# Layer 1's matrices: the second product by even and odd frequencies on row halves, and the root beside it by seed and refinement

## The chip, the cores and the metric

The kernel runs on one core of a Trainium2 chip. The metric is the device time of one execution in microseconds (us), the median over the runs. The engines are TensorE (PE in the profile; PEld is its weight load), VectorE (DVE), ScalarE (ACT), GpSimd (POOL) and SyncE (SP), whose queue issues most DMAs.

## The reference, cut to what matters

Two layers follow each other. Layer 0 takes x of shape 4 x 256 x 256 x 64 through a layer norm, a pointwise product, a two-dimensional Fourier transform, a pointwise layer with gelu, the inverse transform and a depthwise convolution. Layer 1 takes a moving average along the first spatial axis, and filters the rest by one complex matrix for each of 64 channels:

```python
eps = 1e-3                                       # layer 0's norm: (x - mu) * rsqrt(var + eps)
trend = _moving_average(x, KERNEL)               # along T = 256
seasonal = x - trend
xf = jnp.fft.rfft(seasonal, axis=1)
xs = xf[:, :M]                                   # M = 128 frequencies
W = w_real + 1j * w_imag                         # 64 matrices of 128 x 128
ys = jnp.einsum('bmnc,cmk->bknc', xs, W)
filt = jnp.fft.irfft(yf, n=T, axis=1)            # yf is ys with zeros behind it
return trend + filt
```

All of layer 1 is linear in its input, so for each channel c it is one real 256 x 256 matrix: the average, plus (rfft after the removal of the average) x W[c] x (irfft). The kernel computes these 64 matrices itself, since W is an input.

## The kernel before, in words

The whole program is fp32 and runs in stages: a first stage with layer 0's forward transform and most of layer 1's matrices, then the spectral stage, the stages that mix spectrum and convolution, and at the end layer 1 itself, one product per channel with the matrices loaded back from DRAM.

*Forward chunks.* `forward_h` handles chunks of 1024 numbers a partition, 32 for each of the four images. `load` (fl) issues four DMAs into `xt`, which has three buffers. `square` (fq, ScalarE), `add` (fr, VectorE, L283: total), `less_mean` (fR, ScalarE, L288 and L289: mean and sq) and `variance` (fm, VectorE, L294: var) give the statistics; `start_root` (fM) decides on the kind of root, and `root` (fp) makes rstd = (var)^-1/2; `scaled` (fx, GpSimd, L410) multiplies; `halves` (fa, VectorE, L582) and `quarters` (fb, VectorE, L602) form sums and differences; `halves_h` (fh0 and fh1, L609) forms two more, in the first chunks one on GpSimd and one on VectorE, in `xb`, which has one buffer. `transform` (y0, y1, L615) multiplies on TensorE as pairs of 64 columns, and `evict` (yt0, yt1, L633) copies to `yt` and stores to `y_d`.

*Roots.* In this stage `joint["whole"]` is True, and `root` is one GpSimd power (L383) on 128 x 16. Elsewhere in the program it can be a seed from VectorE (L315, an integer operation on the bits of var) and a refinement that alternates between ScalarE and GpSimd in `square_seed`, `first_step`, `square_step` and `root` (fA, fB, fC, fp), called spread.

*Matrices.* `first` (v, L1409 and L1410) multiplies a channel's 128 x 128 real and imaginary weights with tables `f1` and `f2` of 512 columns into one bank. `between` (vc, ScalarE, L1414) copies the bank to `vs`. `second` (mm, L1421) multiplies the two halves of vs with the inverse tables `icr` and `ici` of 256 columns: four products into one bank. `third` (mt, VectorE, L1432) adds the average `avgT` to the bank and stores to `m_d`. 56 channels go this way. The last eight go by halves (hv, hc, hm, ht) beside the spectral stage.

*Order.* TensorE, VectorE, ScalarE and GpSimd run in the order in which the program issues, written out by hand as lists of operations with offsets. `starting` walks the list `FIRST` for 17 periods, each with two chunks and three channels, and from the second period on also a piece of the weight preparation (`prepare`). `BETWEEN` adds five channels and the first steps toward the spectral stage. `do` pulls what an operation follows (`FOLLOWS`), and `make_room` pulls what frees a PSUM bank; there are eight banks, and `NEEDS` says how many an operation takes.

Of the kernel before, what the change touches and what calls it, by code (L numbers as in the profile page):

```python
# [11 lines left out]
F32 = mybir.dt.float32  # L12
I32 = mybir.dt.int32
AF = mybir.ActivationFunctionType
ALU = mybir.AluOpType
# [4 lines left out]
P = 128  # L20
N = 256
C = 64
# [16 lines left out]
def _tables():  # L39

    n = np.arange(N)
# [26 lines left out]
    fr, fi = fr[:, both_halves], fi[:, both_halves]  # L68

# [31 lines left out]
    for par in range(2):  # L101
# [20 lines left out]
        "avgT": fold(avg.T[both_halves]),  # L122
    }
# [13 lines left out]
def conv_seq_kernel(ctx: ExitStack, tc: tile.TileContext, a: dict, tables: bass.AP, out: bass.AP):  # L137
    nc = tc.nc
# [16 lines left out]
    NEEDS = dict(m0=2, m1=2, u=2, s=2, gm=2, em=2)  # L155
# [93 lines left out]
    joint = {"on": False, "open": None, "whole": True}  # L249
# [4 lines left out]
    def statistics(index, src, name, side):  # L254
# [53 lines left out]
        def start_root(j):  # L308
            s = get(j)
            s["whole", side] = joint["whole"] or side == 0 and not joint["on"]  # L310
            s["spread", side] = joint["on"]
            cols = s["cols", side] = None if s["whole", side] else cols_of(s)
            if cols is not None:
                var, seed = s["var"][:, cols], s["seed"][:, cols]
                nc.vector.tensor_scalar(  # L315
                    seed.bitcast(I32), var.bitcast(I32), -0.5, float(0x5F3759DF), ALU.mult, ALU.add
                )
# [1066 lines left out]
    def matrices(pool):  # L1384
# [4 lines left out]
        def table1(name):  # L1389
            return t1[:, _COLS[name][0] - _L1_START : _COLS[name][1] - _L1_START]  # L1390

        f1, f2, icr, ici = (table1(k) for k in ("f1", "f2", "icr", "ici"))
        avgT = table1("avgT")
        CG = 4
# [9 lines left out]
        def first(c):  # L1404
            if c % CG == 0 and c + CG < C:
                load(c + CG)
            ps = pss[c] = bank(f"ps_v_{c}")
            wr, wi = (w[c - c % CG, k][:, c % CG, :] for k in range(2))
            nc.tensor.matmul(ps, wr, f1, start=True, stop=False)  # L1409
            nc.tensor.matmul(ps, wi, f2, start=False, stop=True)  # L1410
# [6 lines left out]
        def second(c):  # L1417
            vs, ps = vss.pop(c), bank(f"ps_m_{c}")
            for t in range(2):
                for r, ic in enumerate((icr, ici)):  # L1420
                    nc.tensor.matmul(  # L1421
                        ps[:, t * N : (t + 1) * N],
                        vs[:, r, t * P : (t + 1) * P],
                        ic,
                        start=r == 0,
                        stop=r == 1,
                    )
            pss[c] = ps

        def third(c):  # L1430
            mt = pool.tile([P, 2, N], F32, tag="mt", name=f"mt_{c}", bufs=3)
            nc.vector.tensor_tensor(mt.rearrange("p t n -> p (t n)"), avgT, pss.pop(c), ALU.add)  # L1432
            free(f"ps_m_{c}")
            nc.sync.dma_start(m_d[c], mt)
# [36 lines left out]
        ops = {"v": first, "vc": between, "mm": second, "mt": third}  # L1471
# [78 lines left out]
    def is_late(j):  # L1550
# [14 lines left out]
        st0 ft0 | st1 ft1 st0 | vc v | mm vc | mt mm | hc hv | hm hc | ht hm  # L1565
# [13 lines left out]
    for line in FOLLOWS.replace("\n", "|").split("|"):  # L1579
# [33 lines left out]
        v:1 mm:-2 fl:1 fM fr fm y0:-2 y1:-2 v:2 mm fq:1 fx:-1 fp fh1:-1 fh0:-1 fm:1 vc:1 yt0:-2 fq:1  # L1613
        y1:-1 mt:-2 fx yt1:-2 fb:-1 mt:-3 fb mt fh1 yt0:-1 fp:1 vc:1 mm:-4 fa:-1 fr:1 fl:2 vc y0:-1
        v:1 fR fR:1 yt1:-1 fh0:-1 fM:1 fa
# [9 lines left out]
    MATRICES = {"v", "vc", "mm", "mt"}  # L1625
# [53 lines left out]
    def period(n):  # L1679
        if any(n - k in chunk_at for k in range(7)):  # L1680
            names = FULL if n < B * FWD + 4 else MIXED if n < CONV_FROM else CONV
        else:
            names = SPECTRUM
        joint["on"], joint["whole"] = names is FULL, names is SPECTRUM
# [17 lines left out]
    with in_order, ExitStack() as right:  # L1702
        with (
# [7 lines left out]
            with ExitStack() as early:  # L1711
# [15 lines left out]
                for k, names in enumerate(BETWEEN, C - BESIDE - len(BETWEEN)):  # L1727
                    do("v", k)
                    do("vc", k)
                    do("mt", k - 1)  # L1730
                    for op, at in names:
                        do(op, S0 - 1 + at)
                do("mt", C - BESIDE - 1)
# [66 lines left out]
```

## Time and profile before

| quantity | value |
|---|---|
| median of 2 runs | 4286.2 us (4285.57 to 4286.83) |
| profiled execution, its own time | 4282.18 us |
| its span, first to last instruction | 4280.0 us |
| mean granted TensorE clock | 0.987 |
| busy over the span: PE, PEld, DVE, ACT, POOL | 96%, 54%, 81%, 69%, 74% |
| first and last start of the second product (L1421) | 17.4 and 315.3 us |
| L1409 / L1410 / L1421, records and median of one | 112 of 592 ns / 112 of 592 ns / 448 of 379 ns |
| L1414 / L1432, instructions and median of one | 56 of 568 ns / 56 of 680 ns |
| L383 over the whole program, instructions and median of one | 41 of 2905 ns |

An fp32 product shows as two records, each with a weight load of its own. [...]in a row of records the next one starts earlier than the last ends, so the time of many is read from their starts. The line numbers are those of the kernel before; in the changed kernel the same functions lie a few lines lower. In the order of time, a line has its start, the time until its end, the engine, line, operation, tiles and number of instructions merged, and in brackets the idle time of the engine before it and what ended it.

### The profile page before, as it was taken

The page shows a single profiled execution, that of the slowest core. Times are in us where ns is not written, and L with a number is a line of the kernel's source. Part 1 is how long each engine was busy: PE and PEld are TensorE (multiplying, and loading weights), DVE is VectorE, ACT ScalarE, POOL GpSimd, SP SyncE. Part 2 cuts the span into 40 slices and gives each one's busy share as a digit, 9 for nine tenths or more (in the row PEclk, how much of TensorE's full clock was granted, in tenths as well). Part 3 has the DMA queues.
Part 4 walks back from the last instruction along what each step waited for, and adds up shares of the span by engine and source line. Part 5 has one row for each costly group of instructions (what it writes and reads, how often), then busy time and mean ns, then how long its engine had stood idle before and what let it go on. Part 6 is the DMA issues. An engine that isn't in the chain of part 4 may idle for free.

```text
span 4280.0 us, 67389 instructions
## 1 busy us (share of the span) xinstructions
PE 4123.3 (96%) x22443; PEld 2329.5 (54%) x22443; DVE 3453.5 (81%) x5234; ACT 2962.3 (69%) x5409; POOL 3174.2 (74%) x3156
## 2 busy tenths in 40 slices
PE   8999999889999999899999999999998899999999
PEld 4544444345555555455555556666665566654444
DVE  6968999889999999899999878888886799962222
ACT  3438988778888887788888777888885466641221
POOL 6869999789999988899988877888886688840000
PEclk9999999999999999999999999999999999999999
DMA  6664555535555545445554333444433544439895
GB/s 192 213 192 132 158 159 165 170 99 138 139 138 138 138 138 141 125 132 140 141 141 133 100 106 101 110 108 123 109 99 101 165 114 114 118 109 368 344 342 226
DMA packets 763904, 655.26 MB, mean 153 GB/s; under 512 B 46413, under 2 KB 657695, under 8 KB 755240
## 3 DMA queue, kind: packets, MB, share of 16 engines
q1 hardware_dynamic: 726696, 583.84, 47.0%
q10 hardware_dynamic: 36864, 67.13, 4.1%
q8 instruction: 180, 2.95, 0.3%
q14 instruction: 164, 1.34, 0.1%
HBM read 364.81 MB, written 286.00 MB: 152 GB/s over the span
## 4 chain that ended last, share of the span: by engine, by line
PE 47%; DVE 8%; DMA 2%; POOL 2%; ACT 1%; issue 1%; SPq 0%; DVEq 0%; POOLq 0%; ACTq 0%
PE ps_o L1504 9%; PE ps_h_c L1166 5%; PE ps_p L750 4%; PE ps_h_c L1180 4%; PE ps_f_c L1283 4%; PE ps_s_c L1041 3%; PE ps_hh_c L1166 3%; PE ps_z L805 3%; PE ps_u L856 2%; PE ps_x L725 2%; PE ps_t_c L1088 2%; PE ps_ft_c L1308 2%; PE ps_hh_c L1180 2%; PE ps_zt L823 1%; PE ps_y L615 1%
## 5 line engine op out<-in xcount | busy, mean ns | idle before, releaser
L770 DVE TENSOR_TENSOR g<-ps_p,g 128x512 f32<-128x512 f32 x1040 | 703.0, 683 | 127.7 <-ACT g L764 109.4
L781 POOL TENSOR_TENSOR g<-g 128x512 f32<-128x512 f32 (+1 forms) x520 | 674.1, 1312 | 92.8 <-ACT g L775 84.9
L775 ACT ACTIVATE g<-g,b_fc 128x1024 f32<-128x1024 f32 (+1 forms) x520 | 595.2, 1145 | 1.7 <-DVE g L770 1.6
L750 PE MATMUL ps_p<-xs,wp 64*128 64x512 f32 (+1 forms) x2080 | 562.2, 615 | 7.0 <-DVE g L770 3.8
L1166 PE MATMUL ps_h_c<-td,wc_main 128*128 128x256 f32 x2048 | 500.5, 387 | 3.7 <-DVE g L770 1.4
L1504 PE MATMUL ps_o<-xc,mt 128*128 128x512 f32 x1024 | 441.2, 594 | 2.6 <-DVE oc L1518 2.6
L1166 PEld LDWEIGHTS ps_h_c<-td,wc_main 128*128 128x128 f32 x2048 | 372.6, 192 | 99.3 <-issue 32.1
L764 ACT COPY g<-ps_p 128x512 f32<-128x512 f32 (+1 forms) x520 | 298.5, 589 | 163.3 <-PE ps_p L750 80.7
L1276 ACT ACTIVATE h_c<-h_c,b_conv 128x1024 f32<-128x1024 f32 x256 | 296.5, 1160 | 158.1 <-DVE h_c L1245 53.8
L1518 DVE TENSOR_SCALAR oc<-ps_o,b_fp 128x512 f32<-128x512 f32 x128 | 93.6, 749 | 348.0 <-DMA out_dram<-oc 177.4
L1516 ACT ACTIVATE oc<-ps_o,b_fp 128x512 f32<-128x512 f32 x128 | 86.4, 686 | 359.4 <-PE ps_o L1504 202.8
L1128 POOL TENSOR_TENSOR td<-tt 128x512 f32<-128x512 f32 x256 | 326.9, 1298 | 10.0
L1504 PEld LDWEIGHTS ps_o<-xc,mt 128*128 128x128 f32 x1024 | 194.9, 191 | 248.3 <-issue 236.2
L609 POOL TENSOR_TENSOR xb<-xt 128x512 f32<-128x512 f32 x224 | 284.9, 1279 | 54.9 <-DVE xt L602 36.6
L750 PEld LDWEIGHTS ps_p<-xs,wp 64*128 64x128 f32 x2080 | 191.7, 186 | 235.7 <-issue 84.2
L805 PE MATMUL ps_z<-g,w_tp 128*64 128x512 f32 x1024 | 284.7, 616 | 25.8 <-POOL g L781 13.9
L1322 DVE TENSOR_TENSOR st<-x_c,ps_ft_c 128x256 f32<-128x256 f32 x512 | 260.5, 599 | 36.9 <-PE ps_ft_c L1308 36.8
L725 PEld LDWEIGHTS ps_x<-tab,yb 128*64 128x64 f32 x4064 | 232.7, 137 | 95.7 <-issue 38.3
L1180 PE MATMUL ps_h_c<-td,wc_half 64*128 64x256 f32 (+1 forms) x2048 | 278.9, 396 | 2.3 <-POOL td L1132 1.0
L615 PE MATMUL ps_y<-xb,tab 128*64 128x512 f32 x1024 | 270.6, 614 | 10.8 <-POOL xb L609 9.2
L1283 PE MATMUL ps_f_c<-h_c,w_fp 128*64 128x512 f32 x1024 | 266.1, 614 | 15.2 <-ACT h_c L1276 15.2
L1041 PE MATMUL ps_s_c<-uc_c,tab 64*128 64x512 f32 x1024 | 260.4, 612 | 16.6 <-DVE uc_c L990 11.2
(201 smaller groups left out, 9588.2 us busy)
## 6 DMA issues: line engine op xcount, KB each, us to landing
y_d<-yt SPq DMA_DIRECT2D x256, 256.0 KB, 3.6
yb<-y_d SPq DMA_DIRECT2D x256, 256.0 KB, 4.2
u_d<-ut SPq DMA_DIRECT2D x256, 256.0 KB, 3.6
x_c<-in_x_dram SPq DMA_DIRECT2D x512, 128.0 KB, 3.6
x_d<-st SPq DMA_DIRECT2D x128, 512.0 KB, 5.1
xc<-x_d SPq DMA_DIRECT2D x64, 1024.0 KB, 8.3
out_dram<-oc ACTq DMA_DIRECT2D x256, 256.0 KB, 5.7
xt<-in_x_dram SPq DMA_DIRECT2D x504, 128.0 KB, 2.5
```

Source lines behind the costliest of these rows:

```text
L725: nc.tensor.matmul(ps[r * C : (r + 1) * C, j * N + t * P : j * N + (t + 1) * P], blk[:, t, k, r * C : (r + 1) * C], tb[:, t, :], start=Tru ...
L750: nc.tensor.matmul(ps[:, :nf], wp[rows, cols], rhs[rows], start=True, stop=r == 1 or not pr["special"],)
L770: nc.vector.tensor_tensor(gt[:, i], re, gt[:, 1], op)
L775: nc.scalar.activation(g, g, AF.Gelu, bias=b_fc[:, half : half + 1])
L781: nc.gpsimd.tensor_tensor(g[:, 0], g[:, 0], g[:, 1], op)
L805: nc.tensor.matmul(ps[r * C : (r + 1) * C, :nf], w_tp, d[:, :nf], start=True, stop=True)
L1041: nc.tensor.matmul(pss[i], tb[i * C : (i + 1) * C], uc[i * C : (i + 1) * C, ::-1, 1 - r, :] if down else uc[i * C : (i + 1) * C, :, r, :], ...
L1128: tt_(new[:, k : k + 3 : 2], a_c, nb_e, op)
L1166: nc.tensor.matmul(product(j, k, par), wc_main[:, par, k, :], td[:, k, slots(j)].rearrange("p j q -> p (j q)"), start=k in (0, 1, 3), stop ...
L1180: nc.tensor.matmul(product(j, k, par)[:, dst.start * Q : dst.stop * Q], wc_half[lo : lo + C, k, :], td[lo : lo + C, k, src].rearrange("p j ...
L1283: nc.tensor.matmul(ps[par * C : (par + 1) * C], w_fp, gs[j][:, :, par, i0 : i0 + 2, :].rearrange("p r j q -> p r (j q)"), start=True, stop ...
L1504: nc.tensor.matmul(ps[:, :nf], mts[i // CM][:, i % CM, t, to * P : (to + 1) * P], xc[:, t, :, :, i, :], start=t == 0, stop=t == 1,)
```

## The change

The irfft's table has a symmetry: half a turn on (T = 256, row n + 128), even frequencies repeat and odd ones change sign. The change uses it in the second product of the 56 channels.

- A table `icp` holds the inverse's first 128 columns with the rows of even frequencies first and those of odd ones after them; it is loaded with the others.
- `first` takes the weights' even and odd columns apart (`s::2`), so that the bank's rows 0 to 63 hold even frequencies and 64 to 127 odd ones: four products of 64 weight columns, in pairs.
- `second` makes eight products of 64 rows by 128 columns, even ones into one bank and odd ones into another (`NEEDS` 2 for mm).
- `odd` (mo) copies the odd bank to SBUF on ScalarE. `third` (mt) adds the even bank, repeated, to the average on VectorE. `fourth` (mu) adds the odd part to one half on VectorE and subtracts it from the other on GpSimd, and stores.
- The roots of the first stage (35 chunks) become seed and spread refinement, by `joint["first"]`, which the first spectral period sets to False.
- `FIRST` is a new list, with mo and mu and with fA, fB, fC in it.

```diff
+    by_parity = np.concatenate([np.arange(0, P, 2), np.arange(1, P, 2)])
+    icp = np.concatenate([icr[by_parity, :P], ici[by_parity, :P]], axis=1)
...
-    NEEDS = dict(m0=2, m1=2, u=2, s=2, gm=2, em=2)
+    NEEDS = dict(mm=2, m0=2, m1=2, u=2, s=2, gm=2, em=2)
...
-    joint = {"on": False, "open": None, "whole": True}
+    joint = {"on": False, "open": None, "whole": False, "first": True}
...
-            s["whole", side] = joint["whole"] or side == 0 and not joint["on"]
-            s["spread", side] = joint["on"]
+            s["whole", side] = joint["whole"] or side == 0 and not (joint["on"] or joint["first"])
+            s["spread", side] = joint["on"] or joint["first"]
...
-            nc.tensor.matmul(ps, wr, f1, start=True, stop=False)
-            nc.tensor.matmul(ps, wi, f2, start=False, stop=True)
+            for k, f in enumerate((f1, f2)):
+                for s in range(2):
+                    nc.tensor.matmul(
+                        ps[s * C : (s + 1) * C],
+                        w[c - c % CG, k][:, c % CG, s::2],
+                        f,
+                        start=k == 0,
+                        stop=k == 1,
+                    )
...
         def second(c):
-            vs, ps = vss.pop(c), bank(f"ps_m_{c}")
+            vs = vss.pop(c)
+            pss[c] = [bank(f"ps_m{k}_{c}")[:, :N] for k in "eo"]
             for t in range(2):
-                for r, ic in enumerate((icr, ici)):
-                    nc.tensor.matmul(
-                        ps[:, t * N : (t + 1) * N],
-                        vs[:, r, t * P : (t + 1) * P],
-                        ic,
...
+                for r in range(2):
+                    for s in range(2):
+                        rows = slice(s * C, (s + 1) * C)
+                        nc.tensor.matmul(
+                            pss[c][s][:, t * P : (t + 1) * P],
+                            vs[rows, r, t * P : (t + 1) * P],
+                            icp[rows, r],
+                            start=r == 0,
+                            stop=r == 1,
+                        )
+
+        def odd(c):
+            turns[c] = pool.tile([P, 2, P], F32, tag="odd", name=f"odd_{c}", bufs=2)
+            nc.scalar.copy(turns[c].rearrange("p t n -> p (t n)"), pss[c].pop())
+            free(f"ps_mo_{c}")
 
         def third(c):
-            mt = pool.tile([P, 2, N], F32, tag="mt", name=f"mt_{c}", bufs=3)
-            nc.vector.tensor_tensor(mt.rearrange("p t n -> p (t n)"), avgT, pss.pop(c), ALU.add)
-            free(f"ps_m_{c}")
-            nc.sync.dma_start(m_d[c], mt)
+            mt = pool.tile([P, 2, 2, P], F32, tag="mt", name=f"mt_{c}", bufs=3)
+            even = pss.pop(c)[0].rearrange("p (t n) -> p t n", t=2)
+            nc.vector.tensor_tensor(
+                mt,
+                avgT.rearrange("p (t h n) -> p t h n", t=2, h=2),
+                even.unsqueeze(2).to_broadcast([P, 2, 2, P]),
+                ALU.add,
+            )
+            free(f"ps_me_{c}")
+            turns[c] = mt, turns[c]
+
+        def fourth(c):
+            mt, o = turns.pop(c)
+            nc.vector.tensor_tensor(mt[:, :, 0], mt[:, :, 0], o, ALU.add)
+            nc.gpsimd.tensor_tensor(mt[:, :, 1], mt[:, :, 1], o, ALU.subtract)
+            nc.sync.dma_start(m_d[c], mt.rearrange("p t h n -> p t (h n)"))
...
-        st0 ft0 | st1 ft1 st0 | vc v | mm vc | mt mm | hc hv | hm hc | ht hm
+        st0 ft0 | st1 ft1 st0 | vc v | mm vc | mo mm | mt mo | mu mt | hc hv | hm hc | ht hm
...
     FIRST = numbered("""
-        v:1 mm:-2 fl:1 fM fr fm y0:-2 y1:-2 v:2 mm fq:1 fx:-1 fp fh1:-1 fh0:-1 fm:1 vc:1 yt0:-2 fq:1
-        y1:-1 mt:-2 fx yt1:-2 fb:-1 mt:-3 fb mt fh1 yt0:-1 fp:1 vc:1 mm:-4 fa:-1 fr:1 fl:2 vc y0:-1
-        v:1 fR fR:1 yt1:-1 fh0:-1 fM:1 fa
+        mt:-3 fl:1 mu:-3 mm:-2 v:1 fm fM y0:-2 y1:-2 v:2 mm fx:-1 fA fB fC fq:1 fx fp fh0:-1 mt:-2
+        fh1:-1 mu:-2 yt1:-2 yt0:-2 vc:1 mo:-2 fM:1 mo mt mu y1:-1 fr:1 fm:1 fb:-1 mo:-3 fB fb fh1
+        fa:-1 vc:1 fh0:-1 fR:1 mm:-4 fr:1 yt0:-1 fA:1 fC:1 fp:1 fl:2 fR vc y0:-1 fq:1 v:1 yt1:-1 fa
     """)
...
-                    do("mt", k - 1)
+                    do("mu", k - 1)
```

## The prediction

> **What bounds the kernel now.** The page's busy shares (TensorE 96%) mix stages, so I first asked for the busy time in stretches of 20 us, to find where the matrices' lines (L1409 to L1434) run: 10 to 316 us and nowhere else. Only this stage can change: 17 periods of two forward chunks and three channels, then a tail of five channels up to the first spectral product at 316.7 us. A middle stretch reads (columns: busy us and count of TensorE, weight loads, VectorE, ScalarE, GpSimd; granted clock, DMA share, GB/s):
>
> ```profile
> 120.00:140.00 20.00, 19.54 (x71) 9.96 (x70) 18.07 (x23) 9.09 (x19) 17.65 (x10) 1.00 0.65 196
> ```
>
> Three engines look full, so the second view is the order of time on VectorE, over one period:
>
> ```profile
> 124.67 1.28 DVE L582 TENSOR_TENSOR xb<-xt 128x512 f32<-128x512 f32 x2
> 125.99 1.29 DVE L602 TENSOR_TENSOR xt<-xb 128x512 f32<-128x512 f32 x2
> 127.20 1.28 DVE L1432 TENSOR_TENSOR mt<-t,ps_m 128x512 f32<-128x512 f32 x2
> 128.40 0.88 DVE L609 TENSOR_TENSOR xb<-xt 128x512 f32<-128x512 f32 x1
> 129.20 1.21 DVE L283 TENSOR_REDUCE total<-xt 128x16 f32<-128x1024 f32 x1
> 130.95 1.25 DVE L294 TENSOR_REDUCE var<-sq 128x16 f32<-128x1056 f32 x1 [0.55 <-ACT sq L289]
> 132.12 1.30 DVE L582 TENSOR_TENSOR xb<-xt 128x512 f32<-128x512 f32 x2
> 133.46 1.29 DVE L602 TENSOR_TENSOR xt<-xb 128x512 f32<-128x512 f32 x2
> 134.78 0.69 DVE L609 TENSOR_TENSOR xb<-xt 128x512 f32<-128x512 f32 x1
> 135.64 1.22 DVE L283 TENSOR_REDUCE total<-xt 128x16 f32<-128x1024 f32 x1 [0.16 <-DMA xt<-in_x_dram]
> 137.40 1.25 DVE L294 TENSOR_REDUCE var<-sq 128x16 f32<-128x1056 f32 x1 [0.55 <-ACT sq L289]
> 138.57 0.68 DVE L1432 TENSOR_TENSOR mt<-t,ps_m 128x512 f32<-128x512 f32 x1
> ```
>
> VectorE starts the next instruction where the last one ends; its only waits are 0.55 us for ScalarE's mean (L289), twice, and 0.16 for a load. Start to start: halves 1.32 and quarters 1.32 a chunk, L609 0.61 to 0.80, total with its wait 1.75, variance 1.17, and 0.60 for each mt: 2 x 6.27 + 3 x 0.60 = 14.3 us. The period from 251.43 to 265.96, which holds no weight preparation, measured 14.53; this one, with 0.96 of preparation, 15.58. VectorE sets the period. TensorE is second: a record of 512 columns takes 0.427 us (two records per fp32 product), so a channel costs 1.71 + 1.71 and a chunk's ps_y 1.71, 13.7 us a period, and up to 14.5 with the 0.15 us seen at each change of tile shape.
>
> Third, the waits on loads and on the power:
>
> ```profile
> L383 POOL TENSOR_TENSOR rstd<-var,minus_half 128x16 f32<-128x16 f32 x33 | 101.5, 3075 | 34.3 <-DVE var L294 34.0
> 64.93 1.28 POOL L609 TENSOR_TENSOR xb<-xt 128x512 f32<-128x512 f32 x1 [2.93 <-DVE xt L602]
> 68.54 0.47 SPq L569 DMA_DIRECT2D xt<-in_x_dram  x1
> 71.51 1.06 ACT L279 ACTIVATE sq<-xt 128x1024 f32<-128x1024 f32 x1 [2.16 <-DMA xt<-in_x_dram]
> ```
>
> The root is 2.9 to 3.1 us of GpSimd a chunk. A chunk's load goes into the buffer that GpSimd's L609 of three chunks before releases: L609 ends at 66.21 and ScalarE's square, which waits for the load, starts at 71.51, 5.3 us later. ScalarE has nothing else to do then, so today it costs nothing.
>
> Fourth, what an idle TensorE costs afterwards:
>
> ```profile
> 302.50 3.68 PE L615 MATMUL ps_y<-xb,tab 128*64 128x512 f32 x8 [4.56 <-POOL xb L609]
> 263.81 1.94 PE L615 MATMUL ps_y<-xb,tab 128*64 128x512 f32 x8
> 3285.26 1.11 PE L1088 MATMUL ps_t_c<-ident,xn_c 128*128 128x128 f32 x4 [3.22 <-POOL xn_c L410]
> 3244.93 0.66 PE L1088 MATMUL ps_t_c<-ident,xn_c 128*128 128x128 f32 x4 [2.97 <-POOL xn_c L410]
> ```
>
> The same eight records take 1.94 after work and 3.68 after 4.56 us of idleness. In the stretches of the order of time that I read, every gap over 3.4 us was followed by half speed; gaps of 2.8 to 3.3 went either way, and nearly all shorter ones were harmless.
>
> **What the Trainium skill says.** "TensorE: Matmul & The Clock Gate" (Part 1) gives the same: about 3.4 us of idleness halve the clock, about 3.4 us of work restore it; the trace agrees (3.68 against 1.94). "TensorEngine Tiling (Array Packing)" (Key Properties; PSUM Pressure) says that different tiles run in parallel, and that row tiles must write different banks, which the even and odd banks do; here 16 records of 64 rows by 256 columns (L1180, 2009.70) take 2.00 us and 32 of L725 take 1.92, hence pairs in parallel. "VectorE: DVE Perf Modes" (tier table) keeps fp32 tensor_tensor at its lowest rate, so an SBUF sum of 256 columns costs what L602's 128x256 row shows, 0.42 (0.34 start to start).
>
> **The change part by part.** *First product*: two products become four of 64 columns in pairs. L615 has this shape: 1.71 a channel, as before. Cost 0.
>
> *Second product*: four of 256 columns become eight of 128 on row halves, 16 records in pairs. At 0.107 (128 columns) to 0.116 (L725) a pair: 0.9 us instead of 1.71. Lower bound of the gain 0 (pairs in series), upper 0.85; I take 0.8, 2.4 a period. It lies off VectorE's chain, so the stage gains nothing from it; it becomes idleness.
>
> *Sums*: VectorE's mt stays 512 wide (0.60), then adds 128x256, 0.34: 3 x 0.34 = 1.02 a period on the chain. ScalarE copies the odd bank, 0.37 (L1453) x 3; GpSimd subtracts 128x256, of which the trace has no row: between 0.64 (half of L609) and 1.28 (all of it); I take 0.67, 2.0 a period.
>
> *Root*: VectorE gets the seed (128x16; L315 shows 0.16 to 0.18, about 0.13 start to start) twice, 0.26. The power goes; in its place come five small ScalarE and four small GpSimd operations in turn. The later stage shows the chain (tile newton_c, from 905.4 to 908.5): 0.25 to 0.45 a hop, 3.0 us in all. GpSimd waits in order through it, so its 2.9 us are not freed.
>
> VectorE's floor therefore rises by 1.28: 15.8 a period without preparation, 16.9 with.
>
> *New order*: two of these chains now hang on other things. In the changed order ScalarE has, inside the root of chunk e+2, the square of chunk e+3 with its load wait; and ahead of the root of e+3 it has the eviction of ps_y of chunk e+1. GpSimd has the half sum of e+1 behind the root and scaling of e+2, and the half sum of e+2 behind the root of e+3. That closes a loop. From the start of GpSimd's half sum of e: 1.28 until it ends; load of e+3 landed and square started 4.4 to 4.9 later (5.9; the 5.3 above held a y_d store queued ahead of it); square and two affine steps 1.65 (7.6); last GpSimd step 0.4 (8.0); scaling 1.9 (9.9); half sum of e+1 1.28 (11.2); ps_y of e+1 1.9 (13.1); eviction 0.55 (13.65); root of e+3 3.0 (16.65); then the half sum of e+2. The loop is 16.5 to 16.9 with a warm TensorE, as long as VectorE's floor.
>
> But TensorE's work before that ps_y, ps_y of e, one first product and two second ones, 1.9 + 1.75 + 1.9 from 1.35 on, ends near 6.9: it then waits 4.0 to 4.5 us for 11.2. Such a gap was always followed by half speed, so ps_y takes about 3.5: the loop becomes 17.9 to 18.7. I take 18.2.
>
> *Store and table*: SP's m_d store now waits for GpSimd too; behind it stand y_d stores and loads, but its sums are over before the load's own condition: 0. The table is 131 KB larger: at 190 GB/s 0.7 us at the start.
>
> *Tail (283 to 317 us)*: TensorE sets it in part, seven second products, some at half speed; the longer way of a channel (copy, add, subtract) and the root's chain give some of it back. Bounds -8 and +1; I take -4.
>
> **Sum.** From the halves of chunk 7 (85.5) to those of chunk 31 (274.25) there are 12 periods of 15.73. 12 x (18.2 - 15.73) = +29.6. The three periods before (16.9 each, waits of preparation in them) +1.3 each: +4. Tail -4, table +0.7: +30. The profiled execution took 4282.2 (span 4280.0): 4312.5. It lay 4.0 under the median of 4286.2: **4316 us**.
>
> **Rivals.** (1) *No half speed*: the gap stays under 3 us, or the load lands sooner; the period is VectorE's floor and the warm loop, 16.8. For: VectorE's chain is nearly without gaps. Against: 4 us of gap. 12 x 1.07 + 4 - 4 + 0.7 = +13.5, **4300**.
> (2) *TensorE was the bound after all*, and its relief pays: for it speaks 19.54 of 20 us busy, and 14.5 of work in periods of 14.5. Then 15 periods lose 2.4: -36, **4250**, not slower. It needs VectorE to absorb 1.28 more, and its list shows at most 0.55 twice that a better order could close; it decides only if VectorE's waits shrink by more than 1.3 a period.
> (3) *Half speed throughout*: if the gaps come so often that the clock never recovers, 11.3 us of TensorE work become 22.6 a period, 12 x 6.9 + 4 = +87, **4373**. Against: after each gap some 8 us of dense work follow.
> (4) *The halves don't run in pairs*: the second product stays at 1.7, the gap shrinks below 3, and the time is that of (1).
>
> **How the numbers follow.** Forecast 0.55, rivals (1) and (4) 0.34, (2) 0.07, (3) 0.04. The range runs from below (1), with a tail of -8 (4294), to the loop at its longest, 18.7, with a tail of +1 and GpSimd's subtractions at the upper bound (4331): 4293 to 4331. Faster by over 2% needs a gain of 86 us, more than the stage could give; within 2% is about what a measurement of this kernel can tell from no change. Faster 0.01, within 0.95, slower 0.04.
>
> **What would show it.** VectorE's period in the order of time, 18 us and not 15.7, with new waits ahead of halves (for ps_y) and total; GpSimd's scaling waiting for ScalarE, ScalarE's square for xt in mid-chain; ps_y of the odd chunk at 3.5 us after a gap of over 4; the second product at 0.9. A period under 16 or all ps_y at 1.9 would make it wrong.

## The result, and the profile after

The changed kernel takes 4355.9 us (4354.7 to 4357.1) against 4286.2: a ratio of 1.0158, 95% interval 1.0142 to 1.0174. It is slower by 70 us; the forecast was 30, and its range ended at +45. The profiled execution took 4357.1 (span 4355.4).

Nearly the whole loss lies where the prediction looked for it: the first spectral product starts at 387.6 us instead of 316.7, and what follows lasts 4.5 us longer in these two traces (3967.8 against 3963.3). Counted by the starts of VectorE's total (L283, now L286) of corresponding chunks: up to one of the first chunks 66.7 before and 75.1 after, +8.4; then 13 periods from 66.68 to 270.49 before (15.68 each) and from 75.07 to 336.85 after (20.14 each), +58.0; then the tail, 46.2 before and 50.8 after, +4.5. Together 70.9. Below, "the 13 turns" are these 13 periods, and the times of experiments over them are counted in the same way.

The same stretch of 20 us as before, in the same columns (busy us and count of TensorE, weight loads, VectorE, ScalarE, GpSimd; clock, DMA share, GB/s):

```profile
120.00:140.00 20.00, 11.06 (x54) 3.87 (x56) 14.38 (x23) 9.44 (x25) 10.67 (x14) 0.83 0.43 129
```

Before, three engines were full. Now none is: this stage is bound by waits. In VectorE's order of time:

```profile
175.55 1.22 DVE L286 TENSOR_REDUCE total<-xt 128x16 f32<-128x1024 f32 x1
177.50 1.25 DVE L297 TENSOR_REDUCE var<-sq 128x16 f32<-128x1056 f32 x1 [0.73 <-ACT sq L292]
178.78 0.37 DVE L318 TENSOR_SCALAR seed<-var 128x16 int32<-128x16 int32 x1
...
182.94 0.42 DVE L1461 TENSOR_TENSOR mt<-mt,odd 128x256 f32<-128x256 f32 x1
183.33 1.22 DVE L286 TENSOR_REDUCE total<-xt 128x16 f32<-128x1024 f32 x1
186.77 1.25 DVE L297 TENSOR_REDUCE var<-sq 128x16 f32<-128x1056 f32 x1 [2.22 <-ACT sq L292]
```

The additions and seeds of the forecast are there, but also a wait of 2.22 for the mean of the odd chunk, where it was 0.55. What VectorE waits for is seen by following one turn of the loop over the engines (order of time, ScalarE, GpSimd and TensorE together):

```profile
175.99 1.27 POOL L612 TENSOR_TENSOR xb<-xt 128x512 f32<-128x512 f32 x1
183.31 1.06 ACT L282 ACTIVATE sq<-xt 128x1024 f32<-128x1024 f32 x1 [2.64 <-DMA xt<-in_x_dram]
185.05 0.22 POOL L400 TENSOR_TENSOR rstd<-newton,rstd 128x16 f32<-128x16 f32 x1 [4.00 <-ACT newton L399]
185.35 1.90 POOL L413 TENSOR_TENSOR xt<-xt,rstd 128x1024 f32<-128x1024 f32 x1
187.20 1.26 POOL L612 TENSOR_TENSOR xb<-xt 128x512 f32<-128x512 f32 x1
188.52 3.68 PE L618 MATMUL ps_y<-xb,tab 128*64 128x512 f32 x8 [5.57 <-POOL xb L612]
192.25 0.59 ACT L636 COPY yt<-ps_y 128x512 f32<-128x512 f32 x1 [2.69 <-PE ps_y L618]
192.73 0.22 ACT L357 ACTIVATE newton<-seed 128x16 f32<-128x16 f32 x1
196.05 1.28 POOL L612 TENSOR_TENSOR xb<-xt 128x512 f32<-128x512 f32 x1
```

This is the loop of the prediction, link by link: half sum, load, square in mid-root, scaling, half sum, ps_y at half speed, eviction, root, next half sum: 20.06 us here. GpSimd, one of the three full engines before, waits 4.00 in the middle of a root for ScalarE, and ScalarE for a load. Before, ScalarE waited for loads and for y_d stores too, and more; the waits of the stage from 20 to 280 us, before (columns: total us, times, longest):

```profile
ACT yt L633 <- DMA y_d<-yt: 64.1, 14, 5.3
ACT sq L279 <- DMA xt<-in_x_dram: 60.0, 15, 13.8
```

and after:

```profile
ACT sq L282 <- DMA xt<-in_x_dram: 29.6, 12, 5.8
ACT yt L636 <- DMA y_d<-yt: 15.6, 5, 3.9
POOL rstd L400 <- ACT newton L399: 49.7, 25, 6.7
```

ScalarE waits less for DMAs than before, and yet these waits now stand in the loop: behind each of them stands a root, and behind the root all of GpSimd.

### The profile page after: what moved, and what is told of

It is laid out like the page before. It is cut to its first block, busy times and chain, and to the rows that moved or that the text cites. A ratio compares the mean times of both kernels' runs of the same rounds, so it can differ in the third digit from the quotient of the medians.

```text
span 4355.4 us, 69350 instructions
## 1 busy us (share of the span) xinstructions
PE 4110.1 (94%) x23115; PEld 2301.0 (53%) x23115; DVE 3496.7 (80%) x5325; ACT 3021.0 (69%) x5640; POOL 3151.5 (72%) x3317
## 3 DMA queue, kind: packets, MB, share of 16 engines
q1 hardware_dynamic: 726696, 583.98, 46.2%
## 4 chain that ended last, share of the span: by engine, by line
PE 46%; DVE 8%; DMA 2%; POOL 2%; ACT 1%; issue 1%; SPq 0%; ACTq 0%; DVEq 0%; POOLq 0%
PE ps_o L1535 9%; PE ps_h_c L1169 6%; PE ps_h_c L1183 4%; PE ps_p L753 4%; PE ps_f_c L1286 4%; PE ps_s_c L1044 4%; PE ps_hh_c L1169 3%; PE ps_z L808 2%; PE ps_t_c L1091 2%; PE ps_ft_c L1311 2%; PE ps_u L859 2%; PE ps_x L728 2%; PE ps_hh_c L1183 2%; PE ps_zt L826 1%; DMA out_dram<-oc 1%
## 5 line engine op out<-in xcount | busy, mean ns | idle before, releaser
L618 PE MATMUL ps_y<-xb,tab 128*64 128x512 f32 x1024 | 290.1, 667 | 79.9 <-POOL xb L612 79.2
```

## The experiments

Each run lists its median and its ratio to runs of the kernel before on the same chip. The signed number behind the ratio is the difference of these two medians in us. Three theories stood at the start. A: the forecast's loop sets the period. B: VectorE's additional work does. C: ScalarE's copy of the odd bank, which has two buffers and waits for GpSimd's subtraction of two channels before (26.1 us of waits from 20 to 280 us), holds ScalarE up.

### First round: parts of the loop

**e1_power**, the root taken back:

```
-    joint = {"on": False, "open": None, "whole": False, "first": True}
+    joint = {"on": False, "open": None, "whole": True, "first": False}
```

> The changed kernel with one thing taken back: layer 1's root is again GpSimd's power (one instruction of about 2.9 us after VectorE's variance); the parity matrices and the changed order stay. Theory A (a loop sets the period of 20 us: load of chunk e+3, ScalarE's square inside the root, the rest of the root, scaling, half sum, ps_y at half speed, eviction, next root): the power waits only for the variance, so the load and the square fall out of the loop, GpSimd's work of 2 x (1.28 + 0.9 + 2.9 + 1.9) + 2.2 us is the rest, 16 to 17 us a period, about 4295 to 4312 us in all. Theory B (VectorE's additional sums, 1.0 to 1.5 us a period, and what waits for them, set it): only the seeds go, about 4350. Theory C (ScalarE's copy of the odd bank, which waits for GpSimd's subtraction of two channels before, holds ScalarE up and everything behind it): the copies stay as they are, about 4350.

Measured: 4364.8 us, 1.0185 (1.0155 to 1.0214), +77. A falls for this kernel, and B and C expected less than this too. Its period is again 20 to 22 us, by another loop: in the changed order GpSimd has a subtraction ahead of the power, and waits for VectorE's sums there, 33.2 us from 20 to 280. And GpSimd and VectorE hold each other up (order of time of each, then the durations of L605 from 100 to 300 us: min, median, max in ns):

```profile
167.26 2.09 POOL L413 TENSOR_TENSOR xt<-xt,rstd 128x1024 f32<-128x1024 f32 x1
167.63 2.87 DVE L605 TENSOR_TENSOR xt<-xb 128x512 f32<-128x512 f32 x2
L605 DVE TENSOR_TENSOR xt<-xb x38: 677/691/2389, 103.0 to 299.3; 128x512 f32<-128x512 f32 x38
```

The first of these two quarters, 0.69 us by the median, lasts 2.27 while GpSimd's scaling runs; the longest of all lasts 2.39. The Trainium skill says so in "SBUF — State Buffer" (Who interferes with whom): a VectorE instruction with two SBUF inputs and a GpSimd instruction that reads SBUF exclude each other, and whichever starts first keeps the other out for its whole length. The trace agrees: the quarter started 0.37 us after the scaling and ended 0.55 us after the scaling's end. (GpSimd's power is an exception, see the last section.) The changed order suits the spread root; with the power in it, it is worse than before.

**e2_old_products**, the matrices taken back, root and order kept (core of the edit):

```
-        ops = {"v": first, "vc": between, "mm": second, "mo": odd, "mt": third, "mu": fourth}
+        ops = {"v": first, "vc": between, "mm": second, "mt": third}
```

> The changed kernel with the matrices taken back: both products and the one sum on VectorE as in the kernel before, the root by seed and refinement and the changed order kept (its two steps for the odd bank and the last sums left out, since there are none). TensorE gets 2.4 us a period more to do, so its gap ahead of ps_y shrinks from 4 to 5.5 us to 1.5 to 3. Theory A: the loop stays but with ps_y at 1.9 instead of 3.7, 16.7 to 18 us a period, about 4305 to 4325 us. Theory B: VectorE's additional sums are gone, period back to about 15.9, about 4290. Theory C: no odd copies, 4290 to 4300.

Measured: 4332.1 us, 1.0109 (1.0079 to 1.0138), +45. Root and order alone make most of the loss, without any of VectorE's additional sums and without an odd copy. B and C fall as the main cause; A's figure of +18 to +38 is too low.

**e3_square_late**, the square of the next chunk behind the root:

```
-        ... fx:-1 fA fB fC fq:1 fx fp fh0:-1 mt:-2
+        ... fx:-1 fA fB fC fp fq:1 fx fh0:-1 mt:-2
```

> The changed kernel with one step moved in the order: ScalarE's square of the next chunk, which waits for that chunk's load, is issued after the root of the chunk before it and not in its middle. Theory A: the load leaves the loop; what is left of it is root 3.2, scaling 1.9, half sum 1.3, ps_y 3.7 at most, eviction 0.6, next root 3.2 and what VectorE adds: 16.9 to 17.5 us a period, about 4302 to 4315 us. Theories B and C: no change, about 4356.

Measured: 4366.7 us, 1.0189 (1.0160 to 1.0219), +79. ScalarE's waits for loads fall to 10.1 us from 20 to 280, and nothing is gained. The odd chunk's scaling now runs beside VectorE's quarters (2.39 us again), and by the trace a loop half sum, sums, subtractions, root, half sum, ps_y, quarters closes at nearly the same length (20.7 us over the 13 turns). A single term of A's loop can't be judged by moving a step: the move makes new meetings.

**e4_fill**, TensorE kept warm:

```
-            for t in range(2):
+            for t in [0, 1] * (5 if c % 3 == 0 else 1):
```

> The changed kernel with more work for TensorE: the second product of every third channel, the last one ahead of the odd chunk's ps_y, is computed five times over into the same banks (about 3.6 us more in the gap, the result unchanged). If half speed after the gap is a term of the loop (theory A), ps_y falls from 3.7 to about 1.95 and the period by about 1.7 us, 4325 to 4332 us. Theories B and C, or a loop in which ps_y isn't a term: no change or some us slower, 4356 to 4365.

Measured: 4349.8 us, 1.0150 (1.0120 to 1.0179), +62; the interval covers that of the changed kernel. The odd chunk's ps_y that I read are at 1.94 now (163.41 us), some of the even chunk's at 3.5 to 3.6 in their place, after gaps of 2.8 to 3.3 us (152.74, 172.82). The 13 turns do get shorter, by 0.9 us each (19.2 instead of 20.1), but the tail, in which two of the five channels carry the filler, takes 59.3 us instead of 50.8 and eats most of it. So in this run half speed is worth about half of its 1.7 us a turn, and not the 3.3 that lie between 20.1 and the 16.8 of rival (1).

### Second round: each half of the change alone

Theory D joins: GpSimd's work in its order, and the mutual exclusion.

**e5_sums_vector**:

```
-            nc.gpsimd.tensor_tensor(mt[:, :, 1], mt[:, :, 1], o, ALU.subtract)
+            nc.vector.tensor_tensor(mt[:, :, 1], mt[:, :, 1], o, ALU.subtract)
```

> The changed kernel with GpSimd taken out of the matrices: the subtraction of the odd half is done by VectorE too, right after its addition. VectorE gets 3 x 0.34 to 0.42 us more a period, GpSimd loses 2.2 to 2.9. Theory A (the loop through load, root, scaling, half sum, ps_y, eviction): neither is a term of it, 4350 to 4360 us. Theory D, formed on the first four runs (GpSimd's subtractions stand in its order ahead of the root and wait for VectorE, and a two-input operation of VectorE and one of GpSimd hold each other up: the 128x256 addition took 0.41 us alone and up to 2.1 beside GpSimd, the 128x256 subtraction 0.72 alone and up to 2.7): several loops of nearly one length, of which this relieves some; 1 to 2 us a period less, 4320 to 4338.

Measured: 4365.7 us, 1.0183 (1.0153 to 1.0212), +78. Relieving GpSimd of its subtractions doesn't help: they fall as the main cause of the changed kernel's loss. The exclusion, D's other half, isn't removed by this run.

**e6_matrices_alone**, power and the order before, with mo and mu put in:

```
-    joint = {"on": False, "open": None, "whole": False, "first": True}
+    joint = {"on": False, "open": None, "whole": True, "first": False}
-        mt:-3 fl:1 mu:-3 mm:-2 v:1 fm fM ...
+        v:1 mm:-2 fl:1 fM fr fm y0:-2 y1:-2 mu:-3 v:2 mm fq:1 fx:-1 fp ... mt:-2 fx yt1:-2 fb:-1 mu:-2 fb mt fh1 ...
```

> The matrices' half of the change alone: both products by parity, the odd bank's copy and the three sums, with the root as GpSimd's power and the steps in the order of the kernel before (the new steps put in: last sums of two channels after GpSimd's half sum of the even chunk, those of the third after the scaling). Theory B or any theory in which only VectorE's work counts: 3 x 0.34 = 1.0 us a period, 17 us, about 4303. Theory D: GpSimd gets 2.2 us a period on top of 13.8 and the two engines hold each other up, period 17.5 to 19, 4315 to 4345. If the order and the root alone made the loss, below 4300.

Measured: 4307.7 us, 1.0048 (1.0029 to 1.0068), +20. The time is what theory B gives for VectorE's additions alone, 17 periods of 1.0, but the trace doesn't show that cause: the period over the 13 turns is 17.6 instead of 15.7, within D's 17.5 to 19; the additions last 0.56 in the mean (0.41 alone) and up to 1.80 (from 100 to 300 us), and GpSimd is as full as VectorE (18.5 and 18.4 of 20 us, the mean of six stretches between 80 and 220 us). So the 20 us belong to the matrices' half as a whole; how they divide between additions, subtractions and exclusion isn't shown. The second product's relief of TensorE (15.9 of 20 us busy, 19.3 before, in the same six) buys nothing, as forecast.

**e7_root_alone**, products, sum and order of the kernel before, the root spread:

```
-        s["whole", side] = joint["whole"] or side == 0 and not joint["on"]
-        s["spread", side] = joint["on"]
+        s["whole", side] = joint["whole"] or side == 0 and not (joint["on"] or joint["first"])
+        s["spread", side] = joint["on"] or joint["first"]
```

> The root's half of the change alone: seed on VectorE and refinement in turns of ScalarE and GpSimd, issued in one piece where the power stood, with the products, the sum and the order of steps of the kernel before. If the hops of the root (0.25 to 0.45 us each, in which GpSimd waits in order for ScalarE, and ScalarE for its own queue) lengthen the loop: period 16.5 to 18.5, 4300 to 4335. If the loss came from the changed order or from the matrices: only the two seeds, 0.3 to 0.7 us a period, 4291 to 4298.

Measured: 4369.8 us, 1.0192 (1.0163 to 1.0222), +82. The root alone costs more than the whole change. The changed order is there for it, and brings it from 82 to the 45 of e2.

**e8_sums_between**, on the kernel before:

```
-        v:1 mm:-2 fl:1 fM fr fm ... fh0:-1 fm:1 vc:1 ... mt:-2 fx yt1:-2 fb:-1 mt:-3 fb mt fh1
+        v:1 mm:-2 fl:1 fR mt:-3 fM fr fm ... fh0:-1 fR:1 mt:-2 fm:1 vc:1 ... fx yt1:-2 fb:-1 fb mt:-1 fh1
```

> The kernel before with two of its three mt sums of a period moved: each stands on VectorE between a chunk's total and its variance, where VectorE waited 0.55 us for ScalarE's mean. Nothing else is changed. If VectorE's chain sets the period of the kernel before, as the prediction says: up to 2 x 0.55 = 1.1 us a period less, 4268 to 4278 us (TensorE's 13.7 to 14.5 a period sets the lower end). If it doesn't: 4283 to 4290.

One thing more is changed than the expectation says: the piece of weight preparation, which stands at the middle of the list, moves two steps ahead with this edit.

Measured: 4281.4 us, 0.9985 (0.9975 to 0.9995), 7 us faster, between the two figures. VectorE's two waits are moved out of the way, but the period hardly follows: over the six turns from 112 us on it is 15.2 instead of 15.5, and over the 13 turns 15.66 instead of 15.68. Its stretch from 160 to 180 us:

```profile
160.00:180.00 20.00, 19.74 (x72) 11.29 (x71) 19.73 (x26) 7.63 (x15) 17.87 (x8) 1.00 0.74 221
```

VectorE and TensorE are full at once. If VectorE set the period before, then by a few tenths of a microsecond over TensorE at most; that it alone did isn't shown.

### Third round: ScalarE's part in the root

Theory S: the root costs because ScalarE carries it, and ScalarE's DMA waits stand in its way.

**e9_root_gpsimd**, e7 with ten operations on GpSimd alone:

```
-        s["spread", side] = joint["on"] or joint["first"]
+        s["spread", side] = joint["on"]
```

> The root alone again (products, sum and order of steps of the kernel before), but the refinement after VectorE's seed is done by GpSimd alone, ten small operations in its own order; ScalarE has no part in it. Theory S, formed on the last four runs (the root alone, shared with ScalarE, cost 82 us because ScalarE's waits for loads and for y_d stores, which held up nothing before, now stand in the root's way): ten operations at 0.22 to 0.30 us are no longer than the power's 2.9, so what is left are two seeds, 0.3 to 0.7 us a period: 4291 to 4300 us. Rival: seed and refinement cost the same wherever they run, because the root starts later or lasts longer: 4330 to 4370.

Measured: 4355.3 us, 1.0161 (1.0140 to 1.0181), +69. By the expectation S falls, but the trace shows that the experiment carried a fault of mine. In the order before, the step that issues the seed did nothing, and stands anywhere (VectorE, then GpSimd, in order of time):

```profile
166.37 1.25 DVE L294 TENSOR_REDUCE var<-sq 128x16 f32<-128x1056 f32 x1 [0.55 <-ACT sq L289]
173.71 0.17 DVE L315 TENSOR_SCALAR seed<-var 128x16 int32<-128x16 int32 x1
173.96 0.21 POOL L333 TENSOR_TENSOR newton<-seed 128x16 f32<-128x16 f32 x1 [6.28 <-DVE seed L315]
```

Every second seed comes 6 us after its variance, behind the next chunk's halves. e7 has the same fault; both are repeated below.

**e10_both**, e6 with the additions between total and variance:

```
-        v:1 mm:-2 fl:1 fM fr fm y0:-2 y1:-2 mu:-3 ... fh0:-1 fm:1 ... fb:-1 mu:-2 fb mt fh1
+        v:1 mm:-2 fl:1 fh0:-2 fR mu:-3 fM fr fm y0:-2 y1:-2 ... fh0:-1 fR:1 mu:-2 fm:1 ... fb:-1 fb mt fh1
```

> The matrices' half alone once more (power as in the kernel before), with VectorE's three 128x256 additions placed where VectorE waits 0.55 us for ScalarE's mean, between a chunk's total and its variance: two in the one gap of a period, one in the other; GpSimd's subtractions move with them. If the loss of 20 us of the matrices alone is VectorE's 3 x 0.34 us and nothing else, the two gaps take up to 0.9 us of it back and TensorE, relieved of 2.4 us a period, doesn't bound as it did in the run with the sums moved: period 15.2 to 15.6, 4278 to 4290 us, as fast as the kernel before or a little faster. If GpSimd bounds (2.2 us more on 13.8, and its scaling now behind a subtraction): 4300 to 4315.

Measured: 4322.0 us, 1.0086 (1.0069 to 1.0103), +35, worse than e6, and on the far side of the figure given for GpSimd as the bound. The subtraction of one channel now stands ahead of GpSimd's scaling. The additions last 0.95 us in the mean (up to 2.12), where e6 has 0.56, and VectorE is busy 19.3 of 20 us in those six stretches: moved beside GpSimd's work they got longer. How much of the loss that makes wasn't taken apart.

**e11_buffers**, the changed kernel with a fourth `xt` and a second `yt` buffer in this stage, from the matrices' pool:

```
+            at = extra[0] if j % 4 == 3 and extra[0] else pool
+            xt = at.tile([P, 2, 4, WH, C], F32, tag="xt", name=f"xt_{j}", bufs=1 if at is not pool else 3)
...
+                at = extra[0] if j % 2 and extra[0] else pool
+                yts[j] = at.tile([P, 2, 2, WH, 2, C], F32, tag="yt", name=f"yt_{j}", bufs=1)
```

> The changed kernel with one buffer more for the loads (four instead of three) and one more for the y_d stores (two instead of one) in this stage, so that ScalarE finds each chunk loaded and each store done. Theories A and S: the term of 4.5 to 6.0 us from the half sum to the square leaves the loop, and the evictions don't wait; what is left is VectorE's floor of 16 to 17 and the chain root, scaling, half sum, ps_y, halves: 17 to 18.5 us a period, 4305 to 4330 us. If other loops of nearly the same length stand behind it, as the run with the late square suggested: 4340 to 4360.

Measured: 4334.7 us, 1.0112 (1.0092 to 1.0133), +48, between the two figures. The period is 18.1 in mid-stage (147.27, 165.49, 183.36, 201.57 are starts of every second total). The two buffers, and with them ScalarE's waits for DMAs, are worth some 21 us of the 70; which buffer brings what wasn't measured. Behind them stands a loop of 18 us.

**e12_after_gpsimd**, the edit of e9 on the changed kernel.

> The changed kernel with the refinement on GpSimd alone after VectorE's seed, as above; matrices by parity and the changed order kept. Theory S with the order as a part of the change that serves the shared root: GpSimd's work is what it was with the power (that run took 4364.8), so 4350 to 4370. If ScalarE's part in the root were the whole of the loss: 4305 to 4320.

Measured: 4341.6 us, 1.0129 (1.0108 to 1.0149), +55. Between the two figures: taking ScalarE out of the root helps by 15 us, freeing it of its waits by 21.

### Fourth round: the root alone, with the seed in its place

**e13_root_seed_early** (on e7) and **e14_gpsimd_seed_early** (on e9), the same edit:

```
-        ... fh1:-1 fh0:-1 fm:1 vc:1 yt0:-2 ...
+        ... fh1:-1 fh0:-1 fm:1 fM:1 vc:1 yt0:-2 ...
```

> The root alone, shared by ScalarE and GpSimd, as in the earlier run (4369.8 us), with one step moved: the odd chunk's seed on VectorE follows its variance at once instead of 6 us later. Theory L (the late seed made that loss): 4291 to 4320 us. Theory S (ScalarE's waits for loads and y_d stores stand in the root's way): the waits of 5 to 6 us in its order remain, 4335 to 4370.

> The root alone, refined by GpSimd alone (4355.4 us), with the same step moved: the odd chunk's seed follows its variance at once. Theory L: ten GpSimd operations of 0.22 to 0.3 us start as early as the power did and last as long: 4288 to 4305 us. If VectorE's operations hold GpSimd's small ones up (0.5 to 0.7 us each beside them in the earlier run): 4310 to 4330. If neither: near 4355.

Measured: e13 4363.3 us, 1.0175 (1.0155 to 1.0195), +76; e14 4317.6 us, 1.0068 (1.0048 to 1.0089), +30. With ScalarE in the root, the late seed was worth almost nothing; without it, 38 us. So ScalarE's part costs 46 us, and S is back: e14 has waits of ScalarE for DMAs as long as e13's (76.2 us for y_d stores and 45.0 for loads from 20 to 300 us), but no root behind them. The +30 that is left in e14 fits the exclusion again: its ten small operations last 0.20 to 0.25 each beside VectorE's reductions and mostly 0.5 to 1.0, at most 1.44, beside its operations with two inputs, so that a root takes 4.85 us in the mean where the power takes 2.9 to 3.3; its seed on VectorE, 0.17 alone, takes 0.93 in the mean (all from 100 to 240 us), up to 1.77 beside the scaling. No run takes the exclusion away, so this is read from the trace and not shown by experiment.

**e15_buffers_fill**, the edits of e11 and e4 together.

> The changed kernel with one buffer more for loads and for y_d stores (4334.7 us), and with the second product of every third channel computed five times over into the same banks, so that TensorE has no long gap ahead of the odd chunk's ps_y. Theory A with the load out of the loop: ps_y at 1.95 instead of 3.7 takes 1 to 1.7 us from each period of 18.1: 4312 to 4323 us. If VectorE or GpSimd in their order set those 18.1 us, not ps_y: 4330 to 4340.

Measured: 4346.7 us, 1.0136 (1.0116 to 1.0156), +59, not faster than e11. In total the filler costs at least what it saves, but the run is no clean test of half speed: three turns, in which the even chunk's ps_y ran at half speed instead (147.6, 168.5 and 190.1 us), took 21.1 to 22.2 us, and the tail takes 56.9 instead of e11's 49.8. The last three of the 13 turns, warm throughout, took 17.0, where e11 has 17.3 to 17.9.

**e16_one_in_three**, e8 with the parity products for every third channel:

```
+            if c % 3 != 2:
+                ... the products and the sum of the kernel before
+                return
```

> The kernel before with the root as power, two mt sums moved between total and variance (4281.4 us, TensorE then busy 20.0 of 20 us), and the parity products for one channel of three only: TensorE gets 0.8 us a period less, VectorE 0.34 to 0.4 more, GpSimd 0.73 more. If TensorE bounds the run with the sums moved, the period falls from 15.2 to 14.5 to 14.8: 4268 to 4277 us. If what a period loses to VectorE, GpSimd and ScalarE's copy comes to as much: 4278 to 4290.

Measured: 4280.8 us, 0.9986 (0.9979 to 0.9993): the time of e8. What TensorE gets back is lost again; the rival figure, that VectorE, GpSimd and ScalarE's copy lose as much, fits (4278 to 4290).

**e17_root_buffers** and **e18_before_buffers**, the edit of e11 on e13 and on the kernel before.

> The root alone, shared by ScalarE and GpSimd, seed early (4363.3 us), with one buffer more for the loads and one more for the y_d stores. Theory S (ScalarE's waits of 5 to 7 us for them stand ahead of the root's steps): most of the 46 us against the root on GpSimd alone go, 4312 to 4335 us. If it is the hops between the two engines that cost: 4350 to 4365.

> The kernel before with the same two buffers. ScalarE's waits of 60 us for loads and 64 us for stores go, but VectorE sets the period and nothing waits for ScalarE: 4283 to 4290 us. Below 4275 would mean that those waits were on the path before the change too.

Measured: e17 4298.7 us, 1.0025 (1.0014 to 1.0037), +11; e18 4278.4 us, 0.9977 (0.9969 to 0.9984), 10 us faster. One buffer more for each is worth 10 us with the power and 66 with the shared root, more than S expected. So 56 of the 76 us that the root costs alone come from its meeting with the waits, as S says. The waits from 20 to 300 us, of e13:

```profile
ACT yt L633 <- DMA y_d<-yt: 57.7, 10, 6.7
ACT sq L279 <- DMA xt<-in_x_dram: 45.8, 13, 6.3
POOL newton L355 <- ACT newton L354: 108.6, 23, 7.7
```

and of e17:

```profile
ACT sq L280 <- DMA xt<-in_x_dram: 7.2, 2, 5.9
POOL newton L356 <- ACT newton L355: 68.3, 31, 7.2
```

The y_d wait is gone from the list, the load wait nearly. The hops between the engines are the same in both, so they don't make those 56; they can be part of the 20 us that still lie between e17 and e18. The two buffers were always added together, so that loads and stores aren't told apart. That e18 gains 10 was not expected: those waits were not wholly free before.

## Why the prediction was wrong, step by step

*What held.* VectorE's chain nearly without gaps was read rightly, and TensorE lies just behind it; that VectorE alone set the period isn't confirmed (e8). The first product costs nothing: its eight records start in four pairs 0.43 us apart (199.15 to 200.43 us), 1.71 in all as forecast. The second product runs in pairs (two of them from 180.89 to 182.7 us, 0.9 each, as forecast) and its gain becomes idleness. The matrices' half costs about what was given for the sums (e6: +20 us, where 17 periods of 1.0 were expected), whether for that reason or not. The loop is the one described, and ps_y of the odd chunk runs at half speed in every one of the 13 turns (3.40 to 3.68). The direction was right.

*The step that failed* is the load's term of the loop: "load of e+3 landed and square started 4.4 to 4.9 later". Over the 13 turns it took 5.57 in the mean, from 4.26 to 8.73, 12 us in all above the 4.65 that the sum used. Part of that the prediction had put at nothing: "SP's m_d store now waits for GpSimd too; behind it stand y_d stores and loads, but its sums are over before the load's own condition: 0." SyncE's queue goes out in order, and in five of the turns other DMAs, mostly stores, still stand ahead of the load when the half sum has ended. In the turn after the one shown, the half sum ends at 197.32:

```profile
195.78 0.92 SPq L1463 DMA_DIRECT2D m_d<-mt  x2
196.79 1.28 SPq L652 DMA_DIRECT2D y_d<-yt  x2
198.17 0.65 SPq L567 DMA_DIRECT2D xt<-in_x_dram  x1
200.48 0.47 SPq L572 DMA_DIRECT2D xt<-in_x_dram  x1
```

The last of its four loads goes out 3.16 us after the half sum, where it is 1.6 in the eight turns without that, and the square starts at 203.70. By these times the late issue makes about half of the 12 us (an estimate: 6.6 us over the five turns). Why the loads also landed later wasn't taken apart.

The other terms, against the prediction: square to half sum 3.96 (3.95); half sum, ps_y, eviction and root 9.33 (8.33), 13 us in all. Of these one turn with weight preparation, 14.06 where the others have 8.94 in the mean, makes 5; eviction with root, 4.00 in the mean for 3.55, makes 6, of which some 2 come from three evictions that waited for a y_d store (131.77, 153.98, 213.34); and ps_y, 3.62 for 3.5, makes 1.6. The sum is 1.28 + 5.57 + 3.96 + 9.33 = 20.1, where 18.2 was forecast: 13 x 1.9 = 25 of the 40 us that were missing.

Behind the number is a wrong question. The prediction took the load's time from one place of the trace before, as a latency, and took off the store that stood ahead of it there. It wrote of ScalarE's wait that it "has nothing else to do then, so today it costs nothing". It saw that the square would come to stand inside a root, but not that with the root all of ScalarE's queue enters the chain, and it didn't ask for SyncE's queue in the same way. The evictions' waits for y_d stores, 64.1 us before and the longest item of the list, aren't mentioned. In the changed kernel they fell to 15.6; in the old order, e13, e17 and e18 show what they and the waits for loads carry together: 66 us with ScalarE in the root, 10 with the power.

*Two smaller terms.* The tail was put at -4 and is +4.5, on the far side of the bounds given for it; it wasn't taken apart. The start was put at about +5 (three periods of 1.3 and the table) and is +8.4. Together 12 of the 40; the rest is in the counting, 13 turns against 12 periods. The seed was priced at 0.13 us, from durations of 0.16 to 0.18, and takes 0.42 in the mean (100 to 240 us); the trace before had warned of it, since the longest of L315's 128 instructions there took 1.24.

*The rivals.* (1) had the loop without half speed; with the odd ps_y warm in nearly every turn, e4 still takes 19.2 a turn, its shortest 17.9, and not 16.8: half speed alone isn't what kept the kernel from (1). (2), TensorE as the bound, gets nothing from its relief (e6, e16), but it was close: in e8 TensorE is as full as VectorE. (3), half speed throughout, would have come near the measured time for the wrong reason: the granted clock is 0.83 in the stretch above, not 0.5. (4) falls, the pairs run.

*What makes the 70.* DMA waits in ScalarE's order 21 (e11); the matrices 20 (e6); the shared root without those waits 20 (e17 against e18, +11 and -10). These were measured in different surroundings, so that their sum of 61 isn't an account: some 9 are left, and the loop of 18 us in e11 wasn't taken apart.

## What to carry to other kernels

Before a step of a critical chain is given to an engine "with room", read the waits of that engine's own queue: a wait of 5 us for a DMA that holds up nothing becomes the chain's wait as soon as the chain passes through the same queue, and a buffer more can be worth more than the step itself. Ask the same of the queue that issues the loads: what stands ahead of a load there is part of its time. One long instruction on GpSimd over 16 columns can be a better neighbour for VectorE than ten short ones (below). And where engines are coupled by in-order queues, look for several loops of nearly one length: taking out a term of the longest then shows only the distance to the next.

## What the hardware did that I had not expected

The exclusion between VectorE and GpSimd, named above by its page, was left out of the prediction's prices. Here it made a 128x512 VectorE operation of 0.69 us last 2.39 (e1) and GpSimd's 128x16 operations of 0.22 last up to 1.44 (e14). The 128x16 seed, an operation with a single SBUF tensor as input, lasted up to 1.77 instead of 0.17 (e14, from 166.62 us on, beside a scaling that ended with it).

GpSimd's power of 2.9 us (74 of them in the whole program, not the 41 of the table above) is another sort of neighbour. It reads SBUF too, so by the page's rule it should keep VectorE's two-input operations out for its whole length. In the kernel before, the order lays VectorE's halves and quarters beside it:

```profile
147.88 3.28 POOL L383 TENSOR_TENSOR rstd<-var,minus_half 128x16 f32<-128x16 f32 x1 [1.25 <-DVE var L294]
147.72 1.30 DVE L582 TENSOR_TENSOR xb<-xt 128x512 f32<-128x512 f32 x2
```

Of 48 halves and 48 quarters from 100 to 284 us none took more than 0.704, and 32 and 27 of them lay wholly within a power; the power took at most 3.28, where a half had begun before it. The measurement decides: in this order the power holds VectorE's operations up by nothing that shows. It is no free neighbour everywhere, though: with the subtractions on GpSimd, in e6 and e10, powers of 4.29 and 4.82 occur.
